# The gate's 1x1 convolution of four gates as one wave of 16 small products

## The chip, the cores and the metric

The kernel runs on one core of a Trainium2 chip. A core has TensorE (PE, matrix products from SBUF into PSUM), VectorE (DVE), ScalarE (ACT), GpSimd (POOL) and SyncE (SP), which here issues nearly all DMAs from one queue, in order. Each engine works through its own instructions in order and waits on semaphores for the others. The metric is the time of one execution on the device in microseconds; lower is better.

## The reference

The input x is [8, 8, 512, 512] (batch, channel, row, column), float32. Two layers follow each other, each x = x + f(groupnorm(x)). The first f is a spectral convolution with 4 x 4 low modes. The second is:

```
cml = 15 steps of a coupled map lattice (a 3x3 depthwise convolution of R*g*(1-g)), clipped
h   = relu(conv3x3(x, Wp) + bp)              # 8 -> 128 channels
nca = sigmoid(conv1x1(h, Wu) + bu)           # 128 -> 8
gin = concat([x, cml, nca])                  # 24 channels
g   = sigmoid(conv1x1(relu(conv3x3(gin, Wg1) + bg1), Wg2) + bg2)   # 24 -> 8 -> 8
f   = g * cml + (1 - g) * nca                # = nca + g * (cml - nca)
```

The change concerns the last two lines, the "gate".

## The kernel before, in words

The batch's 8 elements run in a pipeline. In the ticks of element b, TensorE works on three things: the lattice of element b, the hidden convolution (h, nca) of element b, and "others": the gates of element b-1 and the transform ("spectral", layer 0) of element b+1. A last stretch after element 7 has what is left of its hidden rounds and its 43 gates.

**A tick** (`work`, L1013) has a fixed order. Two lattice steps come first, each on a set of 4 x 32 rows: `convolve` (L524, 48 products of 32x32, three waves of 16) into a pair of PSUM banks twice, then `settle`: VectorE empties the banks (L537), ScalarE squares (L543), and SP exchanges border rows with the neighbouring set (`renew`, L570, L571, L580; L641, L646 for the tail set). Between the two steps stands `others.finish()`. Then `transfers()` issues loads, among them the gates' (`feed`, L902). Then up to two hidden rounds (L723, 12 products each; emptied by ScalarE L729 and VectorE L731), the 3x3 product of at most one gate (`conv`, L793), pieces of the transform (L333, L428, L431, L433), after every second round the hidden 1x1 (L742; its result is emptied by ScalarE L749 or VectorE L751, at last a sigmoid L755, and stored by L758), and the 1x1 of at most one gate (`point`, L810).

**PSUM** is four pairs of two banks: `near` are the two pairs of the first step and the first round, `far` those of the second. The gate's 3x3 goes to `near[0][:, 0]`, the hidden 1x1 to `near[1][:, 0]`, the gate's 1x1 to `near[0][:, 1]`. After two rounds the pairs are reversed, so `near` is used again by the second step of the next tick.

**A gate** is 12 output rows of all 8 channels, so 96 partitions. `load` (L772) takes two tiles of [128, 4, 512]: `gin`, the rows around it of x, cml and nca, for the 3x3 (three DMAs, L778), and `mix`, in whose quarters lie x, cml and nca of the 12 rows (three DMAs, L783). `conv` makes 12 products (four column strips, three shifts), then GpSimd cml - nca (L798), VectorE the scaled x + nca (L799) and the relu out of PSUM into the last quarter of `mix` (L803). A tick later `point` makes three products of 128x32 (L810), ScalarE the sigmoid (L814), GpSimd the product with the difference (L816). Another tick later `finish` adds (L821) and stores the 12 rows with one DMA (L828).

**What sets the order.** The program is written out in one go and kept in the order of the source on every engine (`keep_order`). SBUF's big tiles come from 20 slots; `shared.most` (L1076 to L1079) says how many of them loads for gates and the transform may hold: 8, 5 or 3 by stage, 20 in the last stretch. `feed` loads a gate if two slots are free beyond those that the transform still needs (`kept`), at most two gates ahead (three in the last stretch). A gate's product comes in a later tick than its load. In the last 6 ticks of an element no gate is loaded.

Of the kernel before, what the change touches and what calls it, by code (L numbers as in the profile page):

```python
# [41 lines left out]
P = 128  # L42
C = 8
# [74 lines left out]
def conv_layers(ctx: ExitStack, tc: tile.TileContext, a, out):  # L118
# [77 lines left out]
    gpoint = load("w_g2", [P, GR * C])  # L196
# [118 lines left out]
    def layer0(e, bank):  # L315
# [89 lines left out]
        def close(g, mv):  # L405
# [4 lines left out]
            for c in (2 * g, 2 * g + 1):  # L410
# [3 lines left out]
                def store(c=c, xt=xt):  # L414
                    nc.sync.dma_start(
                        out=e.xn[1 : N + 1, c].rearrange("(p j) w -> p j w", j=4), in_=xt
                    )
                    e.done_with(C + c)
                    e.closed.append(c)
# [345 lines left out]
    class Gate:  # L765


        def __init__(self, e, first):
            self.e, self.first, self.r0 = e, first, min(first, N - GR)

        def load(self):

            r0, self.at = self.r0, now[0]
            self.gin = shared.take([P, 4, N], "gin")
            self.mix = shared.take([P, 4, N], "mix")
            for q, src in enumerate((self.e.xn, self.e.cml, self.e.nca)):
# [3 lines left out]
                    in_=view(src, r0 * C * N, [[N, rows * C], [3 * C * N, 4], [1, N]]),  # L780
                )
            for q, src in enumerate((self.e.xn, self.e.cml, self.e.nca)):
                nc.sync.dma_start(  # L783
                    out=self.mix[: GR * C, q],
                    in_=view(src, (r0 + 1) * C * N, [[N, GR * C], [1, N]]),
                )

        def conv(self, ps):

            gin, (x1, d, ng) = self.gin, (self.mix[: GR * C, q] for q in range(3))  # L790
            for n, (dx, lo, hi, at) in enumerate(SHIFTS):
                for j in range(4):
                    nc.tensor.matmul(  # L793
                        ps[32 * j : 32 * j + 32, lo:hi], gband[:, dx], gin[:, j, at : at + hi - lo],
                        start=(n == 0), stop=(n == 2), tile_position=(0, 32 * j),
                    )

            nc.gpsimd.tensor_tensor(d, d, ng, ALU.subtract)  # L798
            nc.vector.scalar_tensor_tensor(  # L799
                x1, x1, self.e.back[: GR * C, 1:2], ng, ALU.mult, ALU.add  # L800
            )
            shared.drop(gin)
            nc.vector.tensor_scalar(self.mix[:, 3], ps, b_g1, 0.0, ALU.add, ALU.max)  # L803

        def point(self, ps):
            mix = self.mix
            ps = ps[: GR * C]
            for j in range(3):
                at = slice(32 * j, 32 * j + 32)
                nc.tensor.matmul(  # L810
                    ps[at], gpoint[:, at], mix[:, 3], start=True, stop=True,
                    tile_position=(0, 32 * j),
                )
            nc.scalar.activation(mix[: GR * C, 2], ps, AF.Sigmoid, bias=b_g2[: GR * C])  # L814
            d = mix[: GR * C, 1]
            nc.gpsimd.tensor_tensor(d, d, mix[: GR * C, 2], ALU.mult)  # L816

        def finish(self):

            x1, o = (self.mix[: GR * C, q] for q in range(2))  # L820
            nc.vector.scalar_tensor_tensor(  # L821
                o, o, self.e.back[: GR * C, 0:1], x1, ALU.add, ALU.add
            )
            self.store()

        def store(self):
            lo = self.first - self.r0
            nc.sync.dma_start(  # L828
                out=view(
                    out, self.e.b * C * N * N + self.first * N,  # L830
                    [[N, GR - lo], [N * N, C], [1, N]],
                ),
                in_=self.mix[C * lo : GR * C, 1],
            )
            shared.drop(self.mix)

    class Element:


        def __init__(self, b):  # L840
# [12 lines left out]
            self.gates = deque(Gate(self, r) for r in range(0, N, GR))  # L853
# [295 lines left out]
```

## Time and profile before

| | |
|---|---|
| time, median of 3 runs | 9507.76 us (9506.13, 9507.76, 9532.57) |
| the profiled execution: its time / its span | 9539.07 / 9537.3 us |
| TensorE clock granted, mean | 0.981 |
| DMA: bytes, share of the queue's 16 engines | 1326.71 MB, 53.5% |
| read from / written to HBM | 977.48 / 270.61 MB |

How to read the profile: a group line names the source line, engine, operation, tiles out<-in, shape and count; after the bar stand its busy time, the mean of one in ns, and the idle time of the engine just before with what ended most of it. A timeline line has start, length (us), engine, line, operation, count, and in brackets the idle time before it. A float32 product is two instructions on TensorE (two passes). PEld is the loading of weights, which runs beside products.

### The profile page before, as it was taken

How to read it: one execution, taken by the hardware profiler on the slowest of the kernel's cores; microseconds unless marked ns; L12 is line 12 of the kernel's file. 1: busy time of each engine (PE TensorE's matmuls, PEld its weight loads, DVE VectorE, ACT ScalarE, POOL GpSimd, SP SyncE). 2: the span in 40 equal slices, each digit the busy share in tenths (PEclk: the TensorE clock that was granted, in tenths of full speed). 3: DMA queues.
4: the chain of work that ended last, by engine and by line, in shares of the span. 5: the costliest groups of instructions: out<-in, count | busy, mean ns of one | idle time of the engine just before them, and what ended most of it. 6: DMA issues, size and time to landing. Idle time of an engine off the chain costs nothing. (4 is left out here: it accounts for less than half of the span.)

```text
span 9537.3 us, 330619 instructions
## 1 busy us (share of the span) xinstructions
PE 9076.3 (95%) x148976; PEld 4075.3 (43%) x148976; DVE 5572.4 (58%) x5820; ACT 4071.8 (43%) x4285; POOL 1671.2 (18%) x1286
## 2 busy tenths in 40 slices
PE   6999999999999999999999999999999999888999
PEld 3444444444444444444444444444444444333433
DVE  5665566655665556655566555665556655454555
ACT  2444444444444444444444444444434444333432
POOL 2010111112121121211212121021211212122122
PEclk9999999999999999999999999999999999999999
DMA  4241365565555555555555546555464555565288
GB/s 146 87 127 35 90 165 137 148 142 137 157 152 142 140 130 146 160 133 136 153 135 162 146 117 172 131 158 133 120 175 131 156 142 123 138 157 139 70 203 196
DMA packets 626870, 1326.71 MB, mean 139 GB/s; under 512 B 75258, under 2 KB 80762, under 8 KB 597970
## 3 DMA queue, kind: packets, MB, share of 16 engines
q1 hardware_dynamic: 623104, 1304.42, 53.5%
q8 instruction: 1170, 19.17, 0.9%
q14 instruction: 242, 1.98, 0.1%
q10 hardware_dynamic: 2354, 1.14, 0.0%
HBM read 977.48 MB, written 270.61 MB: 131 GB/s over the span
## 5 line engine op out<-in xcount | busy, mean ns | idle before, releaser
L524 PE MATMUL pair<-m,band 32*32 32x512 f32 x103680 | 3719.4, 607 | 208.7 <-issue 124.1
L543 ACT ACTIVATE m<-m 128x1024 f32<-128x1024 f32 x2016 | 2124.5, 1055 | 2438.6 <-DVE m L537 2293.2
L723 PE MATMUL pair<-cols,w_p 32*128 32x511 f32 (+1 forms) x24576 | 2860.0, 603 | 44.8 <-ACT y L749 14.4
L524 PEld LDWEIGHTS pair<-m,band 32*32 32x32 f32 x103680 | 2005.0, 103 | 1856.4 <-issue 1052.5
L537 DVE SCALAR_TENSOR_TENSOR m<-pair,dO 128x1024 f32<-128x1024 f32 x1152 | 1356.6, 1219 | 1218.4 <-PE pair L524 973.3
L723 PEld LDWEIGHTS pair<-cols,w_p 32*128 32x128 f32 x24576 | 1310.0, 186 | 1612.4 <-issue 1158.8
L537 DVE SCALAR_TENSOR_TENSOR m<-pair,dE 128x1024 f32<-128x1024 f32 x1008 | 1187.0, 1219 | 1142.4 <-PE pair L524 902.9
L731 DVE TENSOR_SCALAR h<-pair,b_p 128x1024 f32<-128x1024 f32 x1024 | 1313.0, 1283 | 877.8 <-PE pair L723 873.4
L729 ACT ACTIVATE h<-pair,b_p 128x1024 f32<-128x1024 f32 x1024 | 1140.6, 1114 | 902.5 <-PE pair L723 902.1
L816 POOL TENSOR_TENSOR mix<-mix 96x512 f32<-96x512 f32 x344 | 438.0, 1273 | 4302.2 <-ACT mix L814 4053.3
L742 PE MATMUL pair<-h,w_u 128*32 128x512 f32 x8192 | 1059.1, 610 | 47.6 <-ACT h L729 47.5
L793 PE MATMUL pair<-gin,w_g 128*32 128x511 f32 (+1 forms) x8256 | 964.7, 600 | 4.0 <-DMA gin<-nca 2.0
L798 POOL TENSOR_TENSOR mix<-mix 96x512 f32<-96x512 f32 x344 | 442.2, 1285 | 1423.4 <-DMA mix<-nca 1134.4
L547 POOL TENSOR_SCALAR dO<-dO 128x2048 f32<-128x2048 f32 x72 | 394.5, 5491 | 1009.4 <-DVE m L537 1009.1
L742 PEld LDWEIGHTS pair<-h,w_u 128*32 128x32 f32 x8192 | 244.1, 110 | 698.1 <-issue 329.2
L755 ACT ACTIVATE y<-y,b_u 128x512 f32<-128x512 f32 x256 | 184.8, 722 | 816.9 <-DVE y L751 816.9
L793 PEld LDWEIGHTS pair<-gin,w_g 128*32 128x32 f32 x8256 | 234.5, 110 | 684.6 <-issue 463.1
L749 ACT COPY y<-pair 128x512 f32<-128x512 f32 x256 | 150.1, 586 | 634.4 <-PE pair L742 487.2
L803 DVE TENSOR_SCALAR mix<-pair,b_g 128x512 f32<-128x512 f32 x344 | 258.2, 750 | 263.0 <-PE pair L793 262.5
L810 PE MATMUL pair<-mix,w_g 128*32 128x512 f32 x2064 | 370.7, 605 | 41.9 <-DVE mix L803 38.9
L821 DVE SCALAR_TENSOR_TENSOR mix<-mix,back 96x512 f32<-96x512 f32 x344 | 313.5, 911 | 144.2 <-POOL mix L816 144.2
L516 POOL TENSOR_SCALAR dO<-dO,base 128x512 f32<-128x512 f32 x288 | 208.4, 741 | 1075.6 <-DMA dO<-xn 923.9
(87 smaller groups left out, 2632.2 us busy)
## 6 DMA issues: line engine op xcount, KB each, us to landing
gin<-xn SPq DMA_DIRECT2D x344, 384.0 KB
cols<-xn SPq DMA_DIRECT2D x256, 512.0 KB
x<-in_x SPq DMA_DIRECT2D x120, 1024.0 KB
gin<-cml SPq DMA_DIRECT2D x344, 320.0 KB
gin<-nca SPq DMA_DIRECT2D x344, 320.0 KB
dE<-xn SPq DMA_DIRECT2D x288, 256.0 KB
dO<-xn SPq DMA_DIRECT2D x288, 256.0 KB
mix<-xn SPq DMA_DIRECT2D x344, 192.0 KB
```

The lines of the kernel that those rows point to most:

```text
L524: nc.tensor.matmul(ps[h // 2][32 * t : 32 * t + 32, h % 2], band[at, self.channel(step - 1, h, t), dx], m[at, t, dx : dx + N], start=(n == ...
L537: nc.vector.scalar_tensor_tensor(u[:, at], ps[q], FLOOR, d[:, at], ALU.max, ALU.add)
L543: nc.scalar.square(u[:, at], u[:, at])
L547: nc.gpsimd.tensor_scalar(d, d, 0.5, None, ALU.add)
L723: nc.tensor.matmul(ps[g // 2][:, g % 2, lo:hi], w_p[p, dx, i % 2], self.cols[p, i // 2, at : at + hi - lo], start=(n == 0), stop=(n == 2), ...
L729: nc.scalar.activation(h[:, :2], ps[0], AF.Relu, bias=b_p)
L731: nc.vector.tensor_scalar(h[:, 2:], ps[1], b_p, 0.0, ALU.add, ALU.max)
L742: nc.tensor.matmul(ps[32 * g : 32 * g + 32], w_u[:, r % 4], h[:, g], start=(r == self.hs[0][0]), stop=(r == self.hs[-1][0]), tile_position ...
L793: nc.tensor.matmul(ps[32 * j : 32 * j + 32, lo:hi], gband[:, dx], gin[:, j, at : at + hi - lo], start=(n == 0), stop=(n == 2), tile_positi ...
L798: nc.gpsimd.tensor_tensor(d, d, ng, ALU.subtract)
L810: nc.tensor.matmul(ps[at], gpoint[:, at], mix[:, 3], start=True, stop=True, tile_position=(0, 32 * j),)
L816: nc.gpsimd.tensor_tensor(d, d, mix[: GR * C, 2], ALU.mult)
```

## The change

Four gates become a `Quad`, with a tile each for their nca (`ng`), cml (`d`), x (`x1`) and their four relu results (`relu`); strip j of 32 partitions holds four rows (of which three are used) of all channels, and the tile's middle dimension is the gate. `Gate.load` now takes only `gin`; the quad's three tiles are loaded by `Quad.load` with four DMAs each, nca first, when its four gates' loads are out and slots allow.

`Gate.conv` writes strip j of gate k to partition strip (j + k) mod 4, and its relu goes to `relu[:, k]`. So `Quad.point` can make all 16 products (4 gates x 4 strips) with 32x32 weights, each on its own tile of TensorE, gate k into bank k of the two near pairs. Two sigmoids and two GpSimd products of [128, 2, 512] follow. `Quad.blend` (subtraction on [128, 4, 512], scaled sum in two halves) comes once per quad, ahead of the tick's gate. `Quad.finish` does half a quad per call, and the second half stores it: 12 DMAs, one for each of 4 strips and 3 rows (some more where gates overlap at the element's end). The wave comes a tick or more after the fourth gate's 3x3 and after the blend.

In the tick, `feed` moves from ahead of the rounds to the end, behind the products; the transform's own loads (`others.fetch`) stay where they were. `feed` now asks for one free slot beyond `kept`. The transform may use its last place in all ticks that have no wave.

```diff
-    gpoint = load("w_g2", [P, GR * C])
+    gpoint = load("w_g2", [P, 32])
...
         def load(self):
 
-            r0, self.at = self.r0, now[0]
+            e, self.at = self.quad.e, now[0]
             self.gin = shared.take([P, 4, N], "gin")
-            self.mix = shared.take([P, 4, N], "mix")
...
-            for q, src in enumerate((self.e.xn, self.e.cml, self.e.nca)):
-                nc.sync.dma_start(
-                    out=self.mix[: GR * C, q],
-                    in_=view(src, (r0 + 1) * C * N, [[N, GR * C], [1, N]]),
-                )
 
         def conv(self, ps):
 
-            gin, (x1, d, ng) = self.gin, (self.mix[: GR * C, q] for q in range(3))
+            gin, quad = self.gin, self.quad
             for n, (dx, lo, hi, at) in enumerate(SHIFTS):
                 for j in range(4):
+                    to = 32 * ((j + self.k) % 4)
                     nc.tensor.matmul(
-                        ps[32 * j : 32 * j + 32, lo:hi], gband[:, dx], gin[:, j, at : at + hi - lo],
-                        start=(n == 0), stop=(n == 2), tile_position=(0, 32 * j),
+                        ps[to : to + 32, lo:hi], gband[:, dx], gin[:, j, at : at + hi - lo],
+                        start=(n == 0), stop=(n == 2), tile_position=(0, to),
                     )
-
-            nc.gpsimd.tensor_tensor(d, d, ng, ALU.subtract)
+            shared.drop(gin)
+            if self.k == 0:
+                quad.relu = shared.take([P, 4, N], "relu")
+            nc.vector.tensor_scalar(quad.relu[:, self.k], ps, b_g1, 0.0, ALU.add, ALU.max)
+            quad.convolved, quad.at = quad.convolved + 1, now[0]
+
+    class Quad:
...
+        def load(self):
+
+            src = (self.e.nca, self.e.cml, self.e.xn)[len(self.mix)]
+            t = shared.take([P, 4, N], ("ng", "d", "x1")[len(self.mix)])
+            for j in range(4):
+                nc.sync.dma_start(
+                    out=t[32 * j : 32 * j + 32, : self.n],
+                    in_=view(
+                        src, (self.r0 + 1 + 3 * j) * C * N,
+                        [[N, 32], [GR * C * N, self.n], [1, N]],
+                    ),
+                )
+            self.mix.append(t)
+            self.loaded = now[0]
+
+        def blend(self):
+
+            n, (ng, d, x1) = self.n, self.mix
+            nc.gpsimd.tensor_tensor(d[:, :n], d[:, :n], ng[:, :n], ALU.subtract)
+            for k in (0, 2):
+                k1 = min(k + 2, n)
+                nc.vector.scalar_tensor_tensor(
+                    x1[:, k:k1], x1[:, k:k1], self.e.back[:, 1:2], ng[:, k:k1], ALU.mult, ALU.add
+                )
+            shared.drop(ng)
+            self.blended = True
+
+        def point(self, near):
+
+            n, relu, (_, d, _) = self.n, self.relu, self.mix
+            self.pointed = True
+            for k in (1, 3, 0, 2):
+                for j in range(4 if k < n else 0):
+                    at, to = 32 * ((j + k) % 4), 32 * j
+                    nc.tensor.matmul(
+                        near[k // 2][to : to + 32, k % 2], gpoint[at : at + 32],
+                        relu[at : at + 32, k], start=True, stop=True, tile_position=(at, to),
+                    )
+            for k in (0, 2):
+                k1 = min(k + 2, n)
+                nc.scalar.activation(
+                    relu[:, k:k1], near[k // 2][:, : k1 - k], AF.Sigmoid, bias=b_g2
+                )
+                nc.gpsimd.tensor_tensor(d[:, k:k1], d[:, k:k1], relu[:, k:k1], ALU.mult)
+            shared.drop(relu)
+
+        def finish(self):
+
+            _, d, x1 = self.mix
+            k, k1 = self.shown, min(self.shown + 2, self.n)
             nc.vector.scalar_tensor_tensor(
+                d[:, k:k1], d[:, k:k1], self.e.back[:, 0:1], x1[:, k:k1], ALU.add, ALU.add
             )
+            self.shown = k1
+            if k1 < self.n:
+                return False
+            shared.drop(x1)
+            self.store()
+            return True
...
+        def write(self, d, j, k, k1, r):
+            if r == 3:
+                return
+            to = self.e.b * C * N * N + (self.r0 + GR * k + 3 * j + r) * N
+            for q in range(r, 3):
+                nc.sync.dma_start(
+                    out=view(out, to + (q - r) * N, [[N * N, C], [GR * N, k1 - k], [1, N]]),
+                    in_=d[32 * j + C * q : 32 * j + C * q + C, k:k1],
                 )
...
+        def next_gate(self):
+
+            for quad in self.quads:
+                if quad.gates:
+                    return quad.gates
+                if len(quad.mix) < 3:
+                    return None
+            return self.before.quads and self.before.quads[0].gates
...
+            while e and t >= GATES_FROM and not self.paused:
+                if len(self.loaded) == self.limit or shared.room() <= kept:
                     break
...
+            for quad in self.quads:
+                while not quad.gates and len(quad.mix) < 3 and shared.room() > kept:
+                    quad.load()
...
         point = rounds and e.hidden.n % 2 == 0
+        others.blend()
+        quad = others.point()
         gate = others.gate(near[0][:, 0])
-        others.spectral((far[0], far[1]) if gate else (near[0], far[0] if point else near[1]))
+        if gate or quad:
+            others.spectral((far[0], far[1]))
+        else:
+            others.spectral((near[0], far[0] if point else near[1]))
         if point:
             e.hidden.point(near[1][:, 0])
-        if not others.point(near[0][:, 1]):
+        if quad:
+            quad.point(near)
+        else:
             others.spectral([near[0] if gate or point else near[1]])
+        feed()
         tick()
```

## The prediction

> **What bounds the kernel now.** First the page: engines, then the groups of instructions.
>
> ```profile
> span 9537.3 us, 330619 instructions
> PE 9076.3 (95%) x148976; PEld 4075.3 (43%) x148976; DVE 5572.4 (58%) x5820; ACT 4071.8 (43%) x4285; POOL 1671.2 (18%) x1286
> L816 POOL TENSOR_TENSOR mix<-mix 96x512 f32<-96x512 f32 x344 | 438.0, 1273 | 4302.2 <-ACT mix L814 4053.3
> L810 PE MATMUL pair<-mix,w_g 128*32 128x512 f32 x2064 | 370.7, 605 | 41.9 <-DVE mix L803 38.9
> L821 DVE SCALAR_TENSOR_TENSOR mix<-mix,back 96x512 f32<-96x512 f32 x344 | 313.5, 911 | 144.2 <-POOL mix L816 144.2
> ```
>
> TensorE sets the time. The work to be merged is L810: 344 gates, 6 instructions each (three products, two passes). Then the timeline of one steady tick, from the first L524 (1890.32) to the next (1907.46): 17.14 us.
>
> ```profile
> 1890.32 6.58 PE L524 MATMUL pair<-m,band 32*32 32x512 f32 x192
> 1890.50 0.68 ACT L814 ACTIVATE mix<-pair,b_g 96x512 f32<-96x512 f32 x1 [0.26 <-PE pair L810]
> 1891.26 1.27 POOL L816 TENSOR_TENSOR mix<-mix 96x512 f32<-96x512 f32 x1 [14.18 <-ACT mix L814]
> 1893.73 2.36 DVE L537 SCALAR_TENSOR_TENSOR m<-pair,dO 128x1024 f32<-128x1024 f32 x2 [5.01 <-PE pair L524]
> 1896.00 0.74 DVE L821 SCALAR_TENSOR_TENSOR mix<-mix,back 96x512 f32<-96x512 f32 x1
> 1896.83 5.43 PE L723 MATMUL pair<-cols,w_p 32*128 32x512 f32 x48
> 1896.96 2.36 DVE L537 SCALAR_TENSOR_TENSOR m<-pair,dO 128x1024 f32<-128x1024 f32 x2 [0.22 <-issue]
> ...
> 1904.78 1.90 PE L742 MATMUL pair<-h,w_u 128*32 128x512 f32 x16
> 1905.11 0.75 DVE L803 TENSOR_SCALAR mix<-pair,b_g 128x512 f32<-128x512 f32 x1 [0.81 <-PE pair L793]
> ...
> 1906.50 1.03 PE L810 MATMUL pair<-mix,w_g 128*32 128x512 f32 x6
> 1906.50 0.12 PEld L810 LDWEIGHTS pair<-mix,w_g 128*32 128x32 f32 x3 [0.31 <-issue]
> 1906.75 0.69 DVE L751 TENSOR_TENSOR y<-y,pair 128x512 f32<-128x512 f32 x1 [0.89 <-PE pair L742]
> 1907.46 0.24 PEld L524 LDWEIGHTS pair<-m,band 32*32 32x32 f32 x32 [0.84 <-issue]
> ```
>
> Three things are to be seen. L742's 16 instructions go four at a time, 0.43 us apart, so its last pass starts at 1906.07, call it X; L810's two passes cost 0.86 us and follow without a gap. The result of L742 is out of PSUM only at 1907.44, X + 1.37. And VectorE has no slack between the two sets: the second emptying ends at 1899.32, the second hidden round, 2.57 us behind the first (1896.83), needs those banks at 1899.40.
>
> Last, the stretch after the last set, in timeline and by windows (columns there: length, busy and count of each engine, TensorE's clock, DMA share, GB/s).
>
> ```profile
> 9234.63 1.26 POOL L798 TENSOR_TENSOR mix<-mix 96x512 f32<-96x512 f32 x1
> 9234.70 1.74 DVE L821 SCALAR_TENSOR_TENSOR mix<-mix,back 96x512 f32<-96x512 f32 x1 [3.84 <-POOL mix L816]
> ...
> 9200.00:9300.00 100.00, 100.00 (x888) 36.20 (x886) 55.22 (x51) 33.67 (x39) 24.88 (x20) 1.00 0.88 213
> ```
>
> L821 takes 0.74 us alone, and 1.74 when GpSimd is in a two-input operation: it stands until that ends. DMA is 88% busy there, so it could move some 242 GB/s.
>
> **The change part by part.** A "quad" is four gates; there are 11 per element, 88 in all.
>
> Removed, L810: 344 x 0.86 = 296 us, and the 42 us that TensorE stood before it (the page's 41.9). Together -338.
>
> Added, the wave. L524's loads run 127 in 3.93 us, 32 to a wave: 1.0 us for 16 products in two passes. The change of tile shape moves from before L524 to before the wave and costs nothing; in the last stretch, where no L524 follows, it comes twice (0.1 to 0.8 us more, 11 times). But the wave fills all four banks of the near pairs, and one of them holds L742's result. In the order 1, 3, 0, 2 the last four products write it and can't start before X + 1.4 (on ScalarE, L749, it is X + 1.31). L810 even waits for L803, which reads the other bank of its pair, so I take the wait to be by pair: gate 1 starts early, 3, 0 and 2 behind the result. Either way the next L524 comes at X + 2.4 instead of X + 0.53: 1.9 us a quad, 167 us. Lower end 1.0 a quad (no wait, 88 us); upper end below, with the banks. What is queued behind the wait on TensorE is the next tick.
>
> No row shows products of different row tiles writing one bank at once: L524 and L723 give each row tile its own bank, the wave sends four row tiles to each. If the four went one after another as separate passes, a wave would take 4 x 0.86 = 3.4 us, 2.4 more, 211 us in all; below nothing is excluded, since the products can't take less than the wave of L524. I take the wave, being nearest to L524 in shape, and keep the upper end as a rival. The Trainium skill (TensorEngine Tiling (Array Packing), Restrictions and Gotchas) says that different row tiles can't use the same PSUM bank at the same time; by it the wave would go in four parts and the sum be 211 us higher, and this trace has no case of it.
>
> Moved, the last step of a gate. Four L821 become two of 128x1024; one stands between the two sets' emptyings. ScalarE's result of 1024 takes 1.1 us (L729: 1114 ns) from 0.18 after L524; GpSimd's products of 1024 about 2.5 each (twice 1273), back to back from 1.4 to 6.4. VectorE comes to the sum at 5.8 and stands until 6.4, as in the 1.74 line; the sum itself is 0.74 + 0.53 = 1.27. So the second emptying starts at 7.7 and ends at 10.0 where round 2 wants it at 9.1: 0.9 us on TensorE, in the 77 quads that have sets beside them: 69 us. Ends: 0.3 (GpSimd done in time) to 2.0 (its start late by an L755 and a table load). The second sum lies behind the second emptying, beside round 2: nothing; without that cover it would be 1.27.
>
> Moved, subtraction and scaled sum (L798, L799): once per quad, 4.5 to 5.1 us on GpSimd and 2.5 us on VectorE, ahead of L803 and L751. In a plain tick VectorE is done by 17.3 and its next deadline is 19.7: nothing. Counting the shared slots tick by tick by the rules (gin one slot to its product, relu one until the wave, three mix tiles), I find two places that are worse. While the next element's transform holds four slots, subtraction and wave fall into one tick (19 times): L799's 2.5 us and the transform's own VectorE work (L431 1.21, two L433 0.65) then stand before the L751 that the wave waits for, 3 us where VectorE has it, half of the cases: 28 us. And where room allows, three mix tiles (3 MB) and a gin (1 MB) are issued at once, 16 us at 242 GB/s, and the sums come the next tick: VectorE waits for DMA, some 1.5 us reach TensorE beside the transform, 12 times: 18 us (0 to 60). The count leaves 43 gates in each element's ticks, as now, so none spills over.
>
> The last stretch has 10.63 us ticks and no set to hide behind. The first sum waits for both products of GpSimd (7.7 instead of 4.0), both L731 behind it, so L742 is 0.9 to 1.2 late; the next subtraction waits for its 3 MB and for GpSimd, 2 more in the tick after. 11 x 3.3 = 36 us. The end itself: one more tick, two ScalarE and two GpSimd operations of double size, 14 stores for one: 14 us.
>
> SP's queue. Mix loads are 12 per four gates as now (4 x 3; 0.43 us each). Stores go from 4 to 12 per quad, at 0.57 (L580) to 0.84 us (L828): 7 to 10 us in one piece, between the first and the second set's exchange of rows (L570, L571), with cols and the next gate's loads behind. Loads also move past that exchange to the tick's end. Bytes: 3 MB per quad for 2.25, +65 MB. The first halves have four sets and only some 13 us of slack for these rows; L524's existing waits are 124 us for issue and 37 for rows. I take +40 us (0 to 160: nothing to a doubling of these). ScalarE saves 0.5 us a quad, hidden.
>
> Sum: -338 + 167 + 69 + 28 + 18 + 36 + 14 + 40 = +34 us, on a profiled execution of 9539.07 (span 9537.3), which is 31 above the median; I lay it on the median of 9507.76: 9542.
>
> **The rivals.**
>
> Waits hidden, faster: result and first sum lie elsewhere in the tick than I place them, so that 88 x 0.9, 69 and 28 us vanish: 34 - 79 - 69 - 28 = -142, 9366. For it: TensorE is the bound everywhere and 338 us go. Against: X + 1.37 and 0.08 us of slack are rows. It decides where wave and first sum together cost under 2.0 us a quad instead of 2.8: 62 us less over some 80 quads gives -0.3%.
>
> Banks serialise: +211, 9753. For it only the source's pairing of tile and bank; against it, each 32-partition stripe still sees four banks.
>
> Rows come late: the stores and bursts hold up L570's rows and TensorE's instructions; +120 over my 40: 9662. For it 7 to 10 us of SP in one piece; against it, halves with five sets have a tick more slack.
>
> **How the numbers follow.** 0.3% (28 us) is about what a measurement of this kernel tells from no change. The forecast has 0.55: its own range is 9490 to 9600, and of it 0.38 is slower, 0.14 within, 0.03 faster. Hidden waits 0.25, faster. Late rows 0.12 and serialised banks 0.08, slower. So faster 0.28, same 0.14, slower 0.58. The range runs from the hidden waits' figure to past the late rows', 9360 to 9690; outside are half of the first rival and the banks.
>
> **What would show it.** In the changed trace: ticks without a wave at 16.3 us, a tick with a wave at some 18.2, the one after at 17.2, TensorE's idle time before the wave released by L749 or L751; the first sum's line at 1.3 to 1.9 us with GpSimd busy, and round 2 behind it; in the last stretch, sums released by DMA. Wrong if wave ticks are 17.3 or the next are 16.3 (faster), if the wave's loads spread over 3 us (banks), or if L524's idle time by rows or issue doubles.

## The result and the profile after

The changed kernel takes 10390.21 us (median; 10384.56 to 10397.05), the kernel before beside it 9520.17 (9506.13 to 9535.44): a ratio of 1.091, with a 95% interval of 1.089 to 1.094. Slower was forecast, but at 9542 us, 0.4% above the median it was laid on, and the range ended at 9690. The miss is 848 us. The profiled executions show the same loss: a span of 10386.9 us against 9537.3.

The page of the changed kernel, engines and groups (many lines have moved by one: the lattice's product is L525, the hidden products L724; the gate's 3x3 is L789; the new ones are the GpSimd subtraction L828 and VectorE's scaled sum L831). The last two lines are the lattice's product and the copy of y in the kernel before:

```profile
span 10386.9 us, 330442 instructions
PE 9150.9 (88%) x149664; PEld 4109.9 (40%) x149664; DVE 5548.3 (53%) x5484; ACT 4027.5 (39%) x4117; POOL 1605.4 (15%) x862
L525 PE MATMUL pair<-m,band 32*32 32x512 f32 x103680 | 3869.2, 622 | 666.1 <-DVE relu L796 186.1
L724 PE MATMUL pair<-cols,w_p 32*128 32x511 f32 (+1 forms) x24576 | 2930.3, 606 | 173.1 <-ACT y L750 117.7
L831 DVE SCALAR_TENSOR_TENSOR x<-x,back,ng 128x1024 f32<-128x1024 f32 (+1 forms) x176 | 235.1, 1376 | 574.6 <-DMA x<-xn 423.6
L750 ACT COPY y<-pair 128x512 f32<-128x512 f32 x256 | 150.1, 586 | 989.3 <-DMA nca<-y 502.4
...
L524 PE MATMUL pair<-m,band 32*32 32x512 f32 x103680 | 3719.4, 607 | 208.7 <-issue 124.1
L749 ACT COPY y<-pair 128x512 f32<-128x512 f32 x256 | 150.1, 586 | 634.4 <-PE pair L742 487.2
```

The span grew by 849.6 us. TensorE's idle time (span less busy time) went from 461 to 1236 us, which is +775. Its busy time grew by 75, although work was taken away: the gate's 1x1 fell from 370.7 to 170.0 us of busy time (-201), while the four big groups with unchanged instruction counts (lattice, hidden 3x3, hidden 1x1, gate's 3x3) grew by 150, 70, 13 and 21 (+254). So what was to be saved was saved, and TensorE lost the time by standing, and for a smaller part by running slower. The mean granted clock is 0.943 over the span, against 0.981 before. Added up over the traces, TensorE is busy for 620 us at half clock, against 304 before; half of the difference, 158 us, is what the lower clock adds to the busy time. What adds the other 96 of the 254 us is not shown.

Whom it stood for is in the view of waits by releaser (total us, times, longest):

```profile
PE pair L525 <- DVE relu L796: 186.1, 27, 25.7
PE pair L525 <- ACT y L750: 143.5, 16, 14.1
PE pair L525 <- DVE y L752: 135.2, 19, 16.5
PE pair L724 <- ACT y L750: 117.7, 11, 18.6
PE pair L525 <- issue: 116.1, 55, 7.0
PE pair L429 <- ACT h L730: 107.3, 13, 20.9
PE pair L525 <- DMA m<-m: 39.5, 8, 10.5
```

Relu and y take 0.6 to 0.75 us each. They are not slow, they come late, because their engines stand. VectorE stands 423.6 us in L831 for the x tile (35 times, up to 30.1 us), ScalarE 502.4 us in L750 for the store of the previous y (44 times, up to 24.0). The waits for rows (L525 by m<-m) are those of before, 39.5 against 37.3, and those by issue are no longer than before, 116 against 124.

The wait of L429, a product of the transform, is of another kind; it was 9.1 us before. Five of its 13 times, 18.5 to 20.9 us each, make 97 us. The first of them ends at 2937.02, where ScalarE had stood 12.39 and 7.82 us ahead of the first steps of an element's lattice (L503; the first wait ends on dE<-xn), with the emptying of a hidden round behind them in its order. In the runs below this wait stays at 102 us even with one tile of three and no scaled sum, and is 15 us with the tile loads early. So it goes with the place of the tile loads and hardly with their bytes; how is not shown.

One place where TensorE waits for the relu, in element 7, in time order (TensorE, VectorE, SP and GpSimd; the rest left out):

```profile
8880.58 6.58 PE L525 MATMUL pair<-m,band 32*32 32x512 f32 x192
...
8889.87 2.78 PE L789 MATMUL pair<-gin,w_g 128*32 128x512 f32 x24
8890.00 1.76 SPq L815 DMA_DIRECT2D ng<-nca  x4
...
8892.58 3.41 PE L525 MATMUL pair<-m,band 32*32 32x512 f32 x96
8892.74 8.37 SPq L815 DMA_DIRECT2D d<-cml  x4
8901.81 3.89 SPq L815 DMA_DIRECT2D x<-xn  x4
8906.61 0.34 SPq L759 DMA_DIRECT2D nca<-y  x1
8910.55 4.50 POOL L828 TENSOR_TENSOR d<-d,ng 128x2048 f32<-128x2048 f32 x1 [40.89 <-DMA x<-xn]
8913.39 3.94 DVE L831 SCALAR_TENSOR_TENSOR x<-x,back,ng 128x1024 f32<-128x1024 f32 x2 [22.07 <-DMA x<-xn]
8917.25 0.74 DVE L796 TENSOR_SCALAR relu<-pair,b_g 128x512 f32<-128x512 f32 x1
8918.04 4.92 PE L525 MATMUL pair<-m,band 32*32 32x512 f32 x71 [22.05 <-DVE relu L796]
```

The three tiles are asked for from 8890.00 on. VectorE reaches the scaled sum at once and stands 22.07 us. Behind it, in VectorE's order, is the relu of a gate product that has long been done (L789), and the second lattice step needs the relu's bank: TensorE stands 22.05 us. The y store at 8906.61 lies on SP behind all twelve tile loads. And SP itself is slow: the four DMAs of ng go out in 1.76 us, the four of d need 8.37, and SP's own waits in L815 end on the landing of earlier loads. The same stretch by windows (length, busy and count of PE, PEld, DVE, ACT, POOL; then TensorE's clock, DMA share, GB/s):

```profile
8890.00:8913.39 23.39, 5.98 (x120) 1.96 (x116) 1.29 (x2) 2.06 (x2) 2.84 (x1) 0.69 0.93 185
8918.04:8922.00 3.96, 3.96 (x71) 1.64 (x76) 2.20 (x2) 2.12 (x2) 0.00 (x0) 0.50 0.59 158
```

The DMA engines are 93% busy at 185 GB/s, so little was left to move the tiles faster in this stretch. And after the wait TensorE works at half its clock: 71 instructions of L525 take 4.92 us, where 192 took 6.58 before it.

The small steps went as forecast. A tick without a wave takes 16.29 us. A wave, in a tick that no load disturbs:

```profile
1940.16 1.90 PE L743 MATMUL pair<-h,w_u 128*32 128x512 f32 x16
1941.99 0.15 PEld L844 LDWEIGHTS pair<-relu,w_g 32*32 32x32 f32 x8 [0.84 <-DVE relu L796]
1942.13 0.69 DVE L752 TENSOR_TENSOR y<-y,pair 128x512 f32<-128x512 f32 x1 [0.81 <-PE pair L743]
1942.87 0.21 PEld L844 LDWEIGHTS pair<-relu,w_g 32*32 32x32 f32 x24 [0.73 <-DVE y L752]
1943.08 0.41 PEld L525 LDWEIGHTS pair<-m,band 32*32 32x32 f32 x6
1943.54 6.90 PE L525 MATMUL pair<-m,band 32*32 32x512 f32 x191
```

With X = 1941.45 (the last pass of L743) one gate's 8 weight loads come first, the other 24 wait for L752 until X + 1.42, and the next lattice step follows with its first product at X + 1.63 and the other 191 from X + 2.09. That tick took 17.38 us and the one after it 17.65 (with the first half-sum, 1.67 us long, between the sets): 2.45 us a quad over two plain ticks.

The last stretch, from the end of the last lattice step to the end of the span, took 655.6 us against 486.7:

```profile
9731.30:10386.90 655.60, 480.96 (x3994) 161.71 (x3976) 229.23 (x193) 139.07 (x144) 98.69 (x33) 0.85 0.72 160
```

### The profile page after: what moved, and what is told of

It is laid out like the page before. It is cut to its first block, busy times and chain, and to the rows that moved or that the text cites. A ratio compares the mean times of both kernels' runs of the same rounds, so it can differ in the third digit from the quotient of the medians.

```text
span 10386.9 us, 330442 instructions
## 1 busy us (share of the span) xinstructions
PE 9150.9 (88%) x149664; PEld 4109.9 (40%) x149664; DVE 5548.3 (53%) x5484; ACT 4027.5 (39%) x4117; POOL 1605.4 (15%) x862
## 4 chain that ended last, share of the span: by engine, by line
PE 32%; DMA 14%; SPq 4%; issue 3%; DVE 2%; ACT 2%; POOL 1%; DVEq 0%; ACTq 0%; POOLq 0%
PE pair L525 14%; PE pair L724 10%; PE pair L789 3%; DMA ng<-nca 3%; PE pair L743 3%; DMA x<-xn 2%; DMA gin<-nca 2%; DMA d<-cml 2%; SPq L884 1%; DMA nca<-y 1%; DMA m<-m 1%; DMA dE<-xn 1%; ACT h L730 1%; PE pair L844 1%; POOL d L853 1%
## 5 line engine op out<-in xcount | busy, mean ns | idle before, releaser
L525 PE MATMUL pair<-m,band 32*32 32x512 f32 x103680 | 3869.2, 622 | 666.1 <-DVE relu L796 186.1
L724 PE MATMUL pair<-cols,w_p 32*128 32x511 f32 (+1 forms) x24576 | 2930.3, 606 | 173.1 <-ACT y L750 117.7
L525 PEld LDWEIGHTS pair<-m,band 32*32 32x32 f32 x103680 | 2066.7, 105 | 2325.8 <-issue 1010.8
L724 PEld LDWEIGHTS pair<-cols,w_p 32*128 32x128 f32 x24576 | 1335.4, 187 | 1795.2 <-issue 1186.4
L743 PE MATMUL pair<-h,w_u 128*32 128x512 f32 x8192 | 1072.6, 614 | 45.9 <-ACT h L730 41.1
L789 PE MATMUL pair<-gin,w_g 128*32 128x511 f32 (+1 forms) x8256 | 985.4, 611 | 66.1 <-DMA gin<-nca 49.2
L828 POOL TENSOR_TENSOR d<-d,ng 128x2048 f32<-128x2048 f32 (+1 forms) x88 | 393.4, 4470 | 3415.0 <-DMA m<-m 1545.5
L853 POOL TENSOR_TENSOR d<-d,relu 128x1024 f32<-128x1024 f32 (+1 forms) x176 | 416.4, 2388 | 2440.4 <-issue 1303.6
L789 PEld LDWEIGHTS pair<-gin,w_g 128*32 128x32 f32 x8256 | 240.6, 111 | 763.0 <-issue 579.3
L831 DVE SCALAR_TENSOR_TENSOR x<-x,back,ng 128x1024 f32<-128x1024 f32 (+1 forms) x176 | 235.1, 1376 | 574.6 <-DMA x<-xn 423.6
L750 ACT COPY y<-pair 128x512 f32<-128x512 f32 x256 | 150.1, 586 | 989.3 <-DMA nca<-y 502.4
L743 PEld LDWEIGHTS pair<-h,w_u 128*32 128x32 f32 x8192 | 244.1, 110 | 720.1 <-issue 387.5
L796 DVE TENSOR_SCALAR relu<-pair,b_g 128x512 f32<-128x512 f32 x344 | 257.6, 749 | 465.2 <-PE pair L789 419.0
L860 DVE SCALAR_TENSOR_TENSOR d<-d,back,x 128x1024 f32<-128x1024 f32 (+1 forms) x176 | 270.6, 1538 | 55.7 <-POOL d L853 50.5
```

What stands on the lines that cost most here:

```text
L525: nc.tensor.matmul(ps[h // 2][32 * t : 32 * t + 32, h % 2], band[at, self.channel(step - 1, h, t), dx], m[at, t, dx : dx + N], start=(n == ...
L724: nc.tensor.matmul(ps[g // 2][:, g % 2, lo:hi], w_p[p, dx, i % 2], self.cols[p, i // 2, at : at + hi - lo], start=(n == 0), stop=(n == 2), ...
L743: nc.tensor.matmul(ps[32 * g : 32 * g + 32], w_u[:, r % 4], h[:, g], start=(r == self.hs[0][0]), stop=(r == self.hs[-1][0]), tile_position ...
L789: nc.tensor.matmul(ps[to : to + 32, lo:hi], gband[:, dx], gin[:, j, at : at + hi - lo], start=(n == 0), stop=(n == 2), tile_position=(0, to),)
L828: nc.gpsimd.tensor_tensor(d[:, :n], d[:, :n], ng[:, :n], ALU.subtract)
L853: nc.gpsimd.tensor_tensor(d[:, k:k1], d[:, k:k1], relu[:, k:k1], ALU.mult)
```

## The experiments

Three theories, by what stands. **A**: y's store lies on SP behind the tile loads, and with one buffer for y the next y can't be copied out. **B**: VectorE stands in the scaled sum until the x tile has landed, and relu, y and the lattice's emptyings stand behind it. **C** (added after the first four runs): the burst itself, 3 to 4 MB at the tick's end, is too much for the time until its first use, so that whichever waiter is taken away, another shows. All ratios are to the kernel before, run beside on the same chip (9520 to 9528 us).

**Two buffers for y.**

```diff
-                self.y = wk.tile([P, N], F32, tag="y", name="y", bufs=1)
+                self.y = wk.tile([P, N], F32, tag="y", name="y", bufs=2)
```

(A table of the transform shares another tile's place to make room.)

> Edit: the hidden result y has two buffers instead of one (room made by putting mys into a row tile). Theory A (the store of y stands in SP's queue and in the DMA rings behind the 3 to 4 MB of loads that were moved to the tick's end, and the next y waits for its one buffer): the lines 'ACT y <- DMA nca<-y' (502 us) go to near 0, TensorE's idle time by y and by h falls by some 350 us, time about 9950 to 10050. Theory B (VectorE stands in the scaled sum until x1 has landed): the waits stay with the relu, time above 10250.

Measured 10302.42 us, 1.083 (1.081 to 1.085): 88 us less than the change. TensorE's waits after it:

```profile
PE pair L526 <- DVE relu L797: 191.0, 28, 25.1
PE pair L526 <- DVE y L753: 168.6, 31, 17.3
PE pair L725 <- DVE relu L797: 111.0, 9, 18.4
```

ScalarE's copy is gone from the list, and VectorE takes over: the same burst, the next waiter. A is real but small.

**The scaled sum without x1**, with one and with two y buffers. The sum reads and writes ng in place of x1, so x is left out of the result.

```diff
-                    x1[:, k:k1], x1[:, k:k1], self.e.back[:, 1:2], ng[:, k:k1], ALU.mult, ALU.add
+                    ng[:, k:k1], ng[:, k:k1], self.e.back[:, 1:2], ng[:, k:k1], ALU.mult, ALU.add
```

> Left out: the scaled sum takes nca in place of x and writes it, so that VectorE never waits for x1; all loads, stores and operations stay in number and size. Theory A: VectorE's 424 us at x1 vanish but y still waits for its store, time above 10200. Theory B: idle time by the relu and by y on VectorE (186 and 135 us) vanishes with the half-clock after it, time about 9950 to 10050.

> Both edits (the scaled sum's x left out, y in two buffers). If A and B together are the whole loss, the time is 9500 to 9650, my sum of the other terms; if the bursts of loads cost something else (rows, instructions, SP), it stays above 9750.

Measured 10367.64 (1.089; 1.087 to 1.092) and 10281.17 (1.081; 1.079 to 1.082). These two did not isolate B. Writing ng, the sum must wait for GpSimd's subtraction, which reads ng and waits for d's DMA. With two y buffers VectorE stood 377.4 us for it, 41 times. They tell only that another wait for the same burst costs nearly the same.

**The kernel before with its loads at the tick's end.** Nothing of the wave; only the gates' loads move.

```diff
         def transfers():
-            others.feed(t)
+            others.fetch(t)
...
+        others.feed(t)
         tick()
```

> The kernel before, with only the gates' loads moved behind the tick's products; no merging. Theory A in the form that the move alone does it: 1.6 MB per gate ahead of y's store, slower by 3% or more. If the burst of a quad's tiles is needed, within 1% of before.

Measured 9750.81, 1.025 (1.023 to 1.027). This one move costs 229 us on a kernel without any quad, between the two expectations; of the 199 us between the two profiled spans, 190 lie ahead of the last stretch. TensorE's waits for issue rise from 124 to 205 us, those for gin from 2.0 to 39.6, and 75 us are added to its busy time, at an unchanged mean clock (0.982). What puts off its issue, and what slows its products here, was not settled.

**Without the scaled sum.** With two y buffers, L831 left out altogether (x unscaled, no nca added), all loads kept.

```diff
-            for k in (0, 2):
-                k1 = min(k + 2, n)
-                nc.vector.scalar_tensor_tensor(
-                    x1[:, k:k1], x1[:, k:k1], self.e.back[:, 1:2], ng[:, k:k1], ALU.mult, ALU.add
-                )
             shared.drop(ng)
```

> The changed kernel with two y buffers, and VectorE's scaled sum (x scaled, plus nca) left out altogether: the result holds x unscaled and no nca added. All loads and all other work stay. Theory B (VectorE stands in the scaled sum until the three tiles have landed, and relu, y and the lattice's emptyings stand behind it): TensorE's idle time released by relu, by VectorE's y and by the second round's result, some 470 us with two y buffers, goes; about 9850 us (9750 to 9950). Theory C (the burst of 3 to 4 MB itself: rows, gate loads and stores are late in a full DMA queue, whoever stands): the waits pass to issue, to rows and to gin, the time stays at 10150 or above.

Measured 10001.97, 1.050 (1.048 to 1.052): 300 us less than with two buffers, and still 475 above the kernel before. Between B (9850) and C (above 10150), so each holds in part. Now the burst is seen directly:

```profile
PE pair L526 <- DMA m<-m: 161.2, 18, 19.7
PE pair L526 <- issue: 141.1, 65, 6.7
PE pair L790 <- DMA gin<-nca: 115.0, 33, 17.9
```

Rows cost 161 us (39.5 in the change), gin 115 (49).

**One tile instead of three.** As the last, and only cml's tile is loaded; the subtraction and the last sum read it in place of the other two. Slots, ticks and TensorE's work stay.

```diff
-            for j in range(4):
+            for j in range(4 if len(self.mix) == 1 else 0):
                 nc.sync.dma_start(
                     out=t[32 * j : 32 * j + 32, : self.n],
```

> As the run without the scaled sum, and of the quad's three tiles only cml is loaded (1 MB instead of 3, four DMAs instead of twelve); the tiles of nca and x are taken and given back at the same ticks, the subtraction and the last sum read the cml tile in their place, so nca and x are left out of the result. Schedule and TensorE's work are those of the changed kernel. Theory C: the burst is 2 MB at most, waits for issue, rows and gin go as well: 9500 to 9600 us. Theory B alone: the same as the run with three tiles and no scaled sum, within 50 us.

Measured 9634.24, 1.012 (1.010 to 1.013): loading the two tiles, with the scaled sum already gone, costs 368 us. GpSimd's subtraction then waits for one tile instead of two, and this part is not separated from the bytes. TensorE's waits for rows fall from 161.2 to 61.4 us and those for gin from 115.0 to 62.3. C, nearly as forecast.

**The scaled sum at the tick's end**, with two y buffers, behind relu, y and the rounds.

```diff
             quad.point(near)
...
+        others.scale()
         feed()
```

> The changed kernel with two y buffers, and the scaled sum moved from ahead of the tick's gate to its end, behind relu, y and the hidden rounds. All that is computed is computed. Theory B: the sum comes some 16 us later, when its tiles have mostly landed, so that VectorE stands little: 9800 to 9950 us. Theory C: not under 10150 us.

Measured 10167.94, 1.068 (1.065 to 1.071), 134 us less than with two buffers. VectorE's waits for the x tile fall only from 462.5 us (with two y buffers) to 345.2, and what stands behind them is now other work: the hidden 1x1 waits 106.9 us for VectorE's share of the round, and the rounds 89.7 us for its lattice emptyings.

**The tile loads on GpSimd's queue**, with two y buffers.

```diff
-                nc.sync.dma_start(
+                nc.gpsimd.dma_start(
                     out=t[32 * j : 32 * j + 32, : self.n],
```

> The changed kernel with two y buffers, and the quad's twelve loads issued from GpSimd's queue instead of SP's; all that is computed is computed. If what stands is SP, in order behind the burst (y's store, rows, gate loads): under 10050 us. Theory B: VectorE's scaled sum waits for the same bytes as before, 10200 to 10350 us. If GpSimd is itself held up by issuing, its drives and products come late and the time goes above 10350.

Measured 10216.37, 1.073 (1.071 to 1.074), 86 us less. ScalarE's y waits for no store, as with two buffers on SP's queue:

```profile
L751 ACT COPY y<-pair 128x512 f32<-128x512 f32 x256 | 149.8, 585 | 666.6 <-PE pair L744 656.9 <-DMA cml<-m 4.6 <-DMA m<-m 3.5
L832 DVE SCALAR_TENSOR_TENSOR x<-x,back,ng 128x1024 f32<-128x1024 f32 (+1 forms) x176 | 223.7, 1312 | 414.2 <-DMA x<-xn 288.6 <-issue 57.5 <-DMA m<-m 54.3
```

VectorE still stands 414.2 us ahead of the sum, against 631.0 with the loads on SP, and TensorE's waits for gin rise from 51.0 to 122.8 us: the waits move from one reader to another, and freeing SP takes away a small part of the loss. The Trainium skill (DMA: Bandwidth & Descriptors, Issuing engines are not separate DMA queues) says that transfers started by different engines end on the same 16 DMA engines, and that a second starter saves only starting time. This run agrees in so far as only 86 of some 780 us go; it does not show that these 86 are starting time.

**At most two tiles a tick**, with two y buffers, alone and with the sum at the tick's end.

```diff
-                while not quad.gates and len(quad.mix) < 3 and shared.room() > kept:
-                    quad.load()
+                for _ in range(2):
+                    if not quad.gates and len(quad.mix) < 3 and shared.room() > kept:
+                        quad.load()
```

(`next_gate` lets the next quad's gate in while the third tile is out, if slots allow.)

> The changed kernel with two y buffers, at most two of a quad's three tiles issued in a tick, and a later quad's gate loaded meanwhile where slots allow; all that is computed is computed, bytes are the same. Theory B with C (what counts is how much of the burst is still on its way when the next tick comes): the last burst before a scaled sum is a gate's 1 MB and one tile (1 MB, 8 to 10 us at 200 to 240 GB/s) or two, not three, so that a good part of the 680 us goes that 3 MB cost over 1 MB with no sum (10302 to 9634): 9950 to 10150 us. Bytes alone, whenever they come: 10250 to 10350.

> As the run with two tiles a tick, and the scaled sum at the tick's end as in the earlier run (which gained 134 us). Theory B with C: both waits shrink, 9800 to 9980 us. If the sum at the tick's end only moves VectorE's wait to the next tick's first emptying: as the run with two tiles alone, within 50 us.

Measured 10190.56 (1.070; 1.067 to 1.073) and 10130.40 (1.064; 1.061 to 1.067): 112 us for the smaller burst, where 150 to 350 were expected, and 60 more for the late sum. The last tile is still asked for at the end of one tick and used in the next.

**The tile loads ahead of the hidden rounds.** Now the place: the twelve loads go to where the loads stood before the change, gin stays at the end. A tile asked for there is first used a whole tick later, not half a tick, and where slots are short its three tiles fall into two ticks. `feed_mix` is the loop over the quads' tiles, taken out of `feed`. A quad's first gate also waits a tick where no slot is free.

```diff
         def transfers():
+            others.feed_mix(t)
             others.fetch(t)
```

> The changed kernel with two y buffers, and only the quad's twelve tile loads moved from the tick's end to ahead of the hidden rounds (where the loads stood before the change); the gates' gin stays at the tick's end, and a first gate of a quad waits a tick where no slot is free. All is computed, bytes are the same, the scaled sum stays ahead of the tick's gate but comes nearly a full tick after the issue instead of half a tick. If what costs is the time between the burst's issue and its first use: 9850 to 10050 us, TensorE's idle time released by VectorE's relu and y under 250 us. If it is the bytes in whatever place: over 10200.

> The changed kernel with one y buffer, as the change has it, and the tile loads alone moved ahead of the hidden rounds. If y's store behind the loads costs by itself (some 88 us with the loads at the tick's end): 9790 to 9850 us. If the store only stood behind the burst at the tick's end, as the first theory says, the second buffer is worth little now: 9715 to 9770 us.

Measured with two y buffers 9725.86, 1.023 (1.020 to 1.025), and with one 9766.58, 1.024 (1.020 to 1.028). That is 577 and 624 us less than the same kernels with the loads at the end, for the same bytes and work, and for two buffers less than the 9850 to 10050 expected. Around the same place in the pipeline as above, element 2:

```profile
2090.64 2.04 SPq L816 DMA_DIRECT2D ng<-nca  x4
2095.01 4.14 SPq L816 DMA_DIRECT2D d<-cml  x4
2104.47 0.34 SPq L760 DMA_DIRECT2D nca<-y  x1
...
2108.20 3.47 SPq L816 DMA_DIRECT2D x<-xn  x4
...
2128.34 2.47 DVE L832 SCALAR_TENSOR_TENSOR x<-x,back,ng 128x1024 f32<-128x1024 f32 x2
```

The sum comes 20 us after the x tile was asked for, and has no idle time before it. VectorE's waits for the x tile, with the loads at the tick's end and early:

```profile
DVE x L832 <- DMA x<-xn: 462.5, 40, 31.1
...
DVE x L832 <- DMA x<-xn: 128.8, 17, 14.8
```

TensorE's waits that end on VectorE's relu or y fall with them, from 507 to 157 us in all. The move also parts the tiles from gin and often spreads them over two ticks; how much of the 577 us is owed to that was not separated (at the tick's end, two tiles a tick gave 112). Some 87 are the wait of the transform's product (102.8 to 15.4). The second y buffer, 88 us at the tick's end, is worth 41 here, which the spread of the runs (9722 to 9776) nearly covers.

**On top of that place**: the sum at the tick's end; gin asked for early too, wherever a slot is free.

```diff
             others.feed_mix(t)
+            others.feed(t)
```

> As that run, with the scaled sum at the tick's end. Time between issue and use: 9750 to 9900 us, and the idle time left is that of rows, gin and issue, as in the run without the sum, or less. If the gin loads at the tick's end are what is left, not under 9750, since the kernel before with its loads at the tick's end took 9751.

> As the run with two y buffers and the tile loads ahead of the hidden rounds, and the gates' gin is asked for at that place too, behind the tiles, wherever a slot is free, and at the tick's end only otherwise. All is computed, the bytes are the same. If gin at the tick's end is what is left (TensorE waits 95 us for gin there; the kernel before lost 230 us by the later place): 9560 to 9660 us, with gin's waits under 40 us. If bytes in a full queue are what is left: 9690 to 9760.

Measured 9893.77 (1.039; 1.037 to 1.041) and 9746.30 (1.023; 1.021 to 1.026). The late sum now costs 168 us: TensorE's waits for gin rise from 95.2 to 249.3 us, presumably because the sum holds ng's slot longer. The second edit gains nothing, and TensorE's wait for gin hardly changes (81.6 us). But it hardly moved gin either: in both traces the median time from the issue of a gate's gin to its 3x3 product is 22.4 us, and for a tenth of the gates it is under 12.5 and 12.9. So whether gin's place is part of what is left stays open.

**At that place, without the sum, and without two of the tiles.** The edits are those above, combined.

> Two y buffers, tile loads ahead of the hidden rounds, and VectorE's scaled sum left out (x unscaled, no nca added). If VectorE still standing in the sum (129 us of waits for the x tile in the run with it) is what is left: 9600 to 9640 us. If the sum's waits are covered by now: 9690 to 9730.

> As that run, and only cml's tile is loaded (nca and x left out of the result). If the other 2 MB cost as bytes in the queue: a further 100 us or more below the run with three tiles, near 9500. If place was all: within 40 us of it, and then what is left over the sum of the computing steps lies with gin at the tick's end and in the last stretch.

Measured 9705.63 (1.020; 1.018 to 1.021) and 9417.49 (0.988; 0.987 to 0.990). With the loads early the sum costs 20 us instead of 300. Loading the two tiles still costs 288. Without them, and only then, TensorE's two largest groups are nearly as fast as in the kernel before, on the page:

```profile
PE 8930.7 (95%) x149664; PEld 4094.3 (43%) x149664; DVE 5321.5 (57%) x5308; ACT 4033.5 (43%) x4117; POOL 1504.0 (16%) x862
L526 PE MATMUL pair<-m,band 32*32 32x512 f32 x103680 | 3724.7, 604 | 153.5 <-issue 70.2
L725 PE MATMUL pair<-cols,w_p 32*128 32x511 f32 (+1 forms) x24576 | 2865.3, 600 | 37.4 <-DVE m L539 15.5
```

The runs with two y buffers, side by side (median us):

| tile loads | all | no scaled sum | no sum, one tile of three |
|---|---|---|---|
| at the tick's end | 10302 | 10002 | 9634 |
| ahead of the hidden rounds | 9726 | 9706 | 9417 |

Read along the top row and down: 10390 - 88 (second y) - 300 (VectorE standing in the sum) - 368 (2 MB a quad) - 217 (half a tick more for what is left, 86 of it the wait of the transform's product) = 9417. The causes share one burst and each hides part of the others, so the order matters: the place alone takes off 577, the sum after it only 20. What is shown is that the place of the tile loads makes most of the loss: 577 of the 780 us that the kernel with two y buffers lies above the kernel before. That it does so mainly by too little time between the burst and its first use, in the order of VectorE, is what the waits above show. Of the variants that compute all of the output none beat the kernel before; the best is 2.2% slower. What makes up that rest is not settled. It has 3 MB of tiles a quad, against 2.25 MB of `mix` in the kernel before; by the 288 us for 2 MB, the 0.75 MB more would be some 108 us (an estimate). The last stretch took 576.1 us there and 481.4 without the sum and with one tile (before: 486.7), so some 95 us of the rest lie in that stretch; without the sum alone it is some 20 us shorter, so the greater part goes with the two tiles' loads. No run made the tiles smaller without leaving work out.

## Why the prediction was wrong, step by step

**The step that failed** is the term for the loads: "three mix tiles (3 MB) and a gin (1 MB) are issued at once, 16 us at 242 GB/s, and the sums come the next tick: VectorE waits for DMA, some 1.5 us reach TensorE beside the transform, 12 times: 18 us (0 to 60)". The mechanism was named, the size was off by more than an order of magnitude. VectorE's scaled sum ended 35 waits for the x tile, up to 30.1 us each, and taking the sum away gained 300 us. Three things in it were wrong. The rate: 242 GB/s was read from the last stretch at 88% DMA share, and the burst above moves 185 GB/s at 93%. The start: twelve issues at 0.43 us make 5 us, and in the burst above they took from 8890.0 to 8905.7, so the last tile could not start at once. And the share that reaches TensorE: VectorE was said to have slack until 19.7 "in a plain tick", but behind the sum stands the relu, whose bank the next lattice step needs, so at that place nearly the whole wait arrives (22.07 us on VectorE, 22.05 on TensorE).

**"SP's queue ... +40 us (0 to 160)"** looked for the wrong victim. Rows and issue were to be late; in the changed kernel they are not (39.5 and 116.1 us, as before). y's store was not on the list at all, and with a single y buffer it stopped ScalarE for 502.4 us; a second buffer alone gives 88. That loads at the tick's end cost by themselves was priced at part of these 40; in the kernel before it is 229.

**Terms that were missing.** One is the slower TensorE: +254 us of busy time in four groups with unchanged instruction counts, 158 of them by the lower clock after waits. The sum counted every wait once. Another is the wait of the transform's product (L429), 107.3 us against 9.1.

**What was right, or nearly.** The 1x1's removal: -201 us of busy time (forecast -208: 296 less 88 for the wave). The 42 us that TensorE stood before it did not go: ahead of the wave it stands 37.6. Ticks without a wave: 16.29 (16.3). The tick with a wave and the next: 17.38 and 17.65 us instead of 18.2 and 17.2, together 2.45 us a quad over plain ticks against 2.8. The result of L743 does hold the wave (X + 1.42, forecast X + 1.4), but three gates then need only 0.21 us of weight loads, so the next step begins at X + 1.63, and goes on from X + 2.09, instead of X + 2.4. The first half-sum takes 1.67 us beside GpSimd, as forecast (1.3 to 1.9). The 43 gates fit in each element.

**The last stretch**: forecast +36 and +14, measured +169. With one tile loaded early and no scaled sum, the other steps of the wave in place, it is 481.4 us, 5 less than before. So the computing steps there were overpriced, and the tiles' DMA underpriced.

**The rivals.** *Waits hidden* (9366): the computing part does come out on that side, 9417 with one tile of three, but that run moves 1214 MB against 1327 before and leaves out the scaled sum, so it bounds the gain and does not measure it. *Banks serialise*: not so; see below. *Rows come late* (9662): the nearest in kind, loads late in a queue, but the rows were not the ones to wait, and the place was mainly the scaled sum, not the 12 stores.

## What to carry to other kernels

Before moving loads to a later place, divide the bytes of the whole burst by the rate at which the DMA engines really run when full, add the issue time of a full queue, and compare that with the time until the first instruction that reads them; then name everything that stands behind that instruction in its engine's order, because a wait of an in-order engine can reach the bound engine nearly whole (22.05 of 22.07 us above). Batching four small steps into one saves on the bound engine, but it also turns four loads into one burst: ask for the loads as early as the slots allow, or the burst can cost more than the batch saves, as it did here. When a variant takes one waiter away and the time hardly moves, look for the next one on the same bytes.

## What the runs showed of the hardware

**TensorE's clock after a wait.** In the stretch above TensorE stops at 8896.0; the mean granted clock of 0.69 over 8890.00 to 8913.39 means full clock for about 8.9 us of it, so half clock from some 3 us after the stop. After it resumes at 8918.04 the granted clock is still 0.50 in the whole window to 8922.00. The Trainium skill (TensorE: Matmul & The Clock Gate, Part 1: The HAM clock gate) gives an idle and a busy window of about 3.4 us for the two changes. These rows have some 2.9 us to the drop and more than 4 to the return (8922 to 8923 has 0.63), near that but not at it. Over the run the half clock costs 158 us of busy time more than before, 1.7% of the span, and it goes with the waits: with the waits gone (one tile, loads early) TensorE is busy for 274 us at half clock, and the lattice group is back at 3724.7 us, against 3719.4 before.

**SP behind a burst of loads.** Four DMAs of 256 KB each issue in 1.76 us as the first tile of the burst above, and in 8.37 us as the second, with some 2 MB of loads ahead. SP's waits in front of the tile loads end on the landing of gin and ng (178.5, 148.0 and 114.7 us over the run). Whatever is next on SP stands behind them, as y's store did until 8906.61.

**Four row tiles in one bank.** The wave sends products from four row strips into the same bank, each into partitions of its own. The rival had them in sequence at 2.4 us a wave more; the Trainium skill (TensorEngine Tiling (Array Packing), Restrictions and Gotchas) rules out such use of a bank at one time. A wave that has nothing to wait for inside it shows how it runs:

```profile
8862.46 1.15 PE L844 MATMUL pair<-relu,w_g 32*32 32x512 f32 x32 [0.93 <-DVE relu L796]
8863.73 2.12 ACT L850 ACTIVATE relu<-pair,b_g 128x1024 f32<-128x1024 f32 x2 [1.37 <-PE pair L844]
```

All 32 instructions take 1.15 us, about what a wave of the lattice takes (6.58 us for six), and ScalarE reads the first result 1.27 us after the start; in sequence, by the forecast's sum, they would have needed 3.4. So for products into different partitions of one bank the four row tiles do run at one time, and the measurement decides.
